# Relational graph convolution: loop edges taken from the nodes' own rows, the other edges closed up before the gather

## The chip, the cores and the metric

The kernel runs on one core of one Trainium2 chip. The metric is device time in microseconds (us), the median over runs. All engines of the core work side by side, each through its own instructions in order: TensorE (PE) multiplies matrices, VectorE (DVE) and ScalarE (ACT) work element by element, GpSimd (POOL) here only issues the gathers, and SyncE (SP) issues plain loads and stores.

## The reference, cut to what matters

A graph has 50000 nodes with 128 features each, and 850000 edges sorted by destination; 50000 of them are loops, one from each node to itself. Each edge has one of 16 types. Two layers of a relational graph convolution run one after the other, and the end is a residual and a layer norm:

```python
# one layer: h [50000, 128]; W[r] = sum over 8 bases of w_comp[r, b] * basis[b]
seg = dst * 16 + edge_type
agg = segment_sum(h[src], seg, 50000 * 16).reshape(50000, 16, 128)
msg = einsum('nri,rio->no', agg, W)
h = relu(msg + h @ loop_w + bias)
# after two layers
out = layernorm(x + h)
```

So the loop edges go through the typed matrices like all others, and besides them every node has the product with `loop_w`.

## The kernel before, in words

The edges are cut into tiles of 128 in the order of their destinations: 6641 tiles. Ten tiles (K) make a chunk, 665 chunks (C) per layer. The destinations of a tile lie within 12 nodes (WN), those of a chunk within 128.

A short set-up reads sources and destinations, 1024 tiles at a time (`looked_at`), transposes them on TensorE (L237) so that each edge of a tile has its own partition, and keeps them in SBUF for both layers: `src`, the row to gather, and `key`, the distance of an edge's destination from the first of its tile. It also works out where each chunk's nodes begin (`base_i`), how far the next chunk's are from them (`dist`), where each tile's 12 nodes lie in them (`slot`), and a flag `good` that says whether the edges fit this scheme. If they don't, `summed`, a general and slow path that neither version takes on these inputs, runs instead.

Then, for each layer and each chunk c:

- SP loads `hw`, the 128 rows of the chunk's own nodes (L430), in layer 2 also `xw` (L434).
- POOL gathers the source rows of ten tiles into `g`, one indirect DMA of 128 rows each (`gather`, L156). There are six buffers of ten tiles, so POOL runs up to six chunks ahead. Layer 1 gathers from x, layer 2 from H1, which layer 1 writes.
- Every fourth chunk, `weights` loads the edge types of 40 tiles (`rel`, L355), compares them with the type that each partition stands for (`is_rel`, DVE L364), and multiplies by the table of basis weights: `pm` (PE L367) then holds eight basis weights per edge.
- DVE makes `own`, one-hot over a tile's 12 nodes (L442), and `hot`, its product with `pm` (L449, 128x960).
- TensorE multiplies the gathered rows of each tile by `hot` (`pa`, L460, 128x96), ScalarE copies five tiles at a time to `aT` (L467).
- One chunk later (`finish`, called behind the first five tiles of the next chunk) `slots` sums eight products with the basis matrices (`ps`, L380; copied to SBUF as `slots`, L384), and `nodes_of` puts the 120 slots to their nodes with a one-hot matrix (`own` L390, `pn` L394), adds what the chunk before left for shared nodes (`shift` L397, `pn` L398, `kept` L400), transposes `hw` (`turned`, L163, copy `hT` L165), multiplies it by `loop_w` (`po`, L402), adds the bias (`s`, L404) and adds both (`pn`, L405).
- `ended` applies the relu and stores to H1 (L411, L412), or in layer 2 adds x, applies the norm (`normed`) and stores the output.

An f32 matmul appears in the profile as two instructions on TensorE. The framework sets the order of instructions on each engine when the program is built, and puts the semaphores; nothing is ordered by hand beyond the order of the calls and the numbers of buffers. SP carries loads and stores in one queue; the gathers have POOL's queue to themselves.

Of the kernel before, what the change touches and what calls it, by code (L numbers as in the profile page):

```python
# [31 lines left out]
U8 = mybir.dt.uint8  # L33
AF = mybir.ActivationFunctionType
# [5 lines left out]
P = 128  # L40
# [5 lines left out]
BATCH = 8  # L46
AT = 8
PER = 5
GATHERS = 6
# [9 lines left out]
def tile_rgcn_resnorm(  # L59
# [19 lines left out]
    n_tiles = -(-E // P)  # L79
    C = -(-n_tiles // K)  # L80
    assert D == P and N >= P and edges.shape[0] == 1 and AT * NR == P and PER * NB * WN <= BANK and AT * PER * NB <= BANK and K == 2 * PER and C >= 2 and E % ROW == 0
# [5 lines left out]
    H1 = dram.tile([N, D], F32, name="H1")  # L87

# [9 lines left out]
    fixed = ps_c.tile([P, 2, P], F32, name="fixed")  # L98
# [54 lines left out]
    ps_m = ctx.enter_context(tc.tile_pool(name="ps_m", bufs=2, space=PSUM))  # L153
# [20 lines left out]
    n_first = 0  # L174


    n_batches = -(-n_tiles // (P * BATCH))
    src = consts.tile([P, n_batches * P * BATCH], I32, name="src")
    key = consts.tile([P, n_batches * P * BATCH], F32, name="key")
# [3 lines left out]
    slot = consts.tile([P, C], F32, name="slot")  # L183
    good = consts.tile([1, 1], I32, name="good")
    with tc.tile_pool(name="meta1", bufs=1) as m1, tc.tile_pool(name="meta", bufs=2) as mp:
        ones = m1.tile([P, P], F32, name="ones")
        nc.vector.memset(ones, 1.0)

        def looked_at(i):

            raw = mp.tile([P, 2, BATCH, P], I32, name="raw")
            e0 = i * P * BATCH * P
            whole, part_of = divmod(min(E - e0, P * BATCH * P), BATCH * P)
            flat = raw.rearrange("p j b e -> p j (b e)")
            if whole < P:

                nc.vector.memset(flat[:, 0, :], 0)
                nc.vector.memset(flat[:, 1, :], N)
            for j in range(2):
                if whole:  # L200
                    nc.sync.dma_start(flat[:whole, j, :], column(j, e0, [[BATCH * P, whole], [1, BATCH * P]]))
                if part_of:
                    nc.sync.dma_start(
                        flat[whole : whole + 1, j, :part_of],
                        column(j, e0 + whole * BATCH * P, [[part_of, 1], [1, part_of]]),
                    )
            return raw

        raw = looked_at(0)

        first_i = m1.tile([K, C], I32, name="first_i")
        nc.vector.memset(first_i, N)
        with nc.allow_non_contiguous_dma(reason="one word in P"):
            nc.scalar.dma_start(first_i[:, : n_tiles // K], column(1, 0, [[P, K], [K * P, n_tiles // K], [1, 1]]))
            if n_tiles % K:
                nc.scalar.dma_start(  # L216
                    first_i[: n_tiles % K, C - 1 :],
                    column(1, (C - 1) * K * P, [[P, n_tiles % K], [1, 1], [1, 1]]),
                )
        picked = m1.tile([P, n_batches + 2], F32, name="picked")  # L220
        nc.vector.memset(picked, 0.0)
        for i in range(n_batches):
            if i:
                raw = looked_at(i)
            tb = mp.tile([P, BATCH], F32, name="tb")
            nc.vector.tensor_scalar(tb, raw[:, 1, :, 0], float(N - WN), None, op0=OP.min)
            rel0 = mp.tile([P, BATCH, P], F32, name="rel0")
            nc.vector.tensor_tensor(rel0, raw[:, 1], tb[:, :, None].to_broadcast([P, BATCH, P]), op=OP.subtract)
            srcf = mp.tile([P, BATCH, P], F32, name="srcf")
            nc.scalar.copy(srcf, raw[:, 0])  # L230
            t0 = i * P * BATCH
            for of, to in ((srcf, src), (rel0, key)):
                at = to[:, t0 : t0 + P * BATCH].rearrange("e (p b) -> e b p", b=BATCH)
                for b0 in range(0, BATCH, BANK // P):
                    tp = ps_a.tile([P, BANK], F32, name="pa")
                    for b in range(BANK // P):
                        nc.tensor.transpose(tp[:, b * P : (b + 1) * P], of[:, b0 + b, :], ident)  # L237
                    nc.scalar.copy(at[:, b0 : b0 + BANK // P, :], tp.rearrange("e (b p) -> e b p", p=P))
            while n_first < min(GATHERS, C - 1) and (n_first + 1) * K <= (i + 1) * P * BATCH:
                for k in range(K):  # L240
                    gather(rows[n_first][:, k, :], x, src[:, n_first * K + k : n_first * K + k + 1])
                n_first += 1
            own = mp.tile([P, BATCH, P], F32, name="own")
            nc.vector.tensor_scalar(own, rel0, 0.0, None, op0=OP.is_ge)
            nc.vector.scalar_tensor_tensor(
                own.rearrange("p b e -> p (b e)"),
                rel0.rearrange("p b e -> p (b e)"),
                float(WN),
                own.rearrange("p b e -> p (b e)"),
                op0=OP.is_lt,  # L250
                op1=OP.mult,
                accum_out=picked[:, i : i + 1],
            )
        tile_base = m1.tile([K, C], F32, name="tile_base")
        nc.vector.tensor_scalar(tile_base, first_i, float(N - WN), None, op0=OP.min)
        base1 = m1.tile([1, C], F32, name="base1")
        nc.vector.tensor_scalar(base1, tile_base[0:1], float(N - P), None, op0=OP.min)
        nc.vector.memset(base1[:, 0:1], 0.0)
        nc.vector.memset(base1[:, C - 1 :], float(N - P))
        nc.vector.tensor_copy(base_i, base1)  # L260

        spread = m1.tile([K, S], F32, name="spread")
        nc.gpsimd.iota(
            spread, pattern=[[1, S]], base=0, channel_multiplier=-WN, allow_small_or_imprecise_dtypes=True
        )
        ahead = m1.tile([K, S], F32, name="ahead")
        nc.vector.tensor_scalar(ahead, spread, 0.0, None, op0=OP.is_ge)
        nc.vector.scalar_tensor_tensor(spread, spread, float(WN), ahead, op0=OP.is_lt, op1=OP.mult)
        base = m1.tile([P, C], F32, name="base")
        within = m1.tile([P, 1], F32, name="within")  # L270
        po = ps_o.tile([P, D], F32, name="po")
        nc.tensor.matmul(po[:S, :1], spread, part[:K, :], start=True, stop=True)
        nc.vector.scalar_tensor_tensor(
            within[:S], po[:S, :1], float(-WN), part[:S], op0=OP.mult, op1=OP.add
# [58 lines left out]
    def chunked():  # L333
        with tc.tile_pool(name="hp", bufs=2) as hp, tc.tile_pool(
# [12 lines left out]
            def weights(c, n):  # L347
# [4 lines left out]
                if whole < AT:  # L352
                    nc.vector.memset(rel, NR)
# [270 lines left out]
    with tc.If(every > 0) as found:  # L624
        chunked()
# [41 lines left out]
```

## Time and profile before

| | us |
|---|---|
| median of 10 runs | 16696.05 (16694.3 to 16697.5) |
| profiled execution | 16664.61 |
| its span, first to last instruction | 16662.6 |
| POOL busy | 12559.0 |
| PE busy, weight loads | 13016.9, 11184.0 |
| DVE busy, ACT busy | 4001.6, 3111.7 |
| mean granted TensorE clock | 0.677 of full speed |

The busy time of an engine counts its instructions, and for the gathers POOL's own work only: the rows land later, under the DMA's name. A TensorE instruction's end is modelled, so its busy time is rough. The granted clock says how fast TensorE was let run. A group row of the profile gives the line, the engine, the operation, the tiles written and read, how often, busy us and mean ns; behind the second bar the idle time of the engine just before, and what ended it ("issue" if nothing that the profile shows). Times in a timeline are us from the start of the span. The DMA engines were busy for 20.6% with the gathers and 6.8% with SP's transfers.

### The profile page before, as it was taken

What the parts mean: (1) busy time and instruction counts of PE and PEld (TensorE: products, weight loads), DVE (VectorE), ACT (ScalarE), POOL (GpSimd) and SP (SyncE); (2) the same over time, 40 slices, a digit from 0 to 9 for tenths busy, and PEclk for the clock granted to TensorE, in tenths of its full rate; (3) what the DMA queues carried; (4) which work ended last, traced back from release to release, by engine and by line L of the source; (5) the groups of instructions that cost most, each with busy time, mean ns of one, the idle gap of its engine ahead of it and who ended that gap; (6) DMA issues with size and microseconds to landing.
All of it is one profiled execution on the core that took longest, in us unless ns stands there. A gap on an engine that the chain in (4) does not pass through costs nothing.

```text
span 16662.6 us, 191086 instructions
## 1 busy us (share of the span) xinstructions
PE 13016.9 (78%) x60630; PEld 11184.0 (67%) x60630; DVE 4001.6 (24%) x11719; ACT 3111.7 (19%) x8680; POOL 12559.0 (75%) x13290
## 2 busy tenths in 40 slices
PE   6777777777777777777777777778877787877788
PEld 5666666666666666666666666666666666666666
DVE  2222222222222222222222222222222222222222
ACT  2111111111111111111112122222222222222222
POOL 7777777777777777777777777777777777777777
PEclk7766666666666666666666666666666666666666
DMA  3222222222222222222222222222222222222222
GB/s 87 72 70 70 71 70 70 71 70 70 71 70 70 71 70 70 71 70 70 69 75 75 75 76 75 75 76 75 75 76 75 75 76 76 75 76 75 75 76 68
DMA packets 961778, 1218.82 MB, mean 73 GB/s; under 512 B 275684, under 2 KB 704100, under 8 KB 960768
## 3 DMA queue, kind: packets, MB, share of 16 engines
q0 software_dynamic: 425024, 871.30, 20.6%
q1 hardware_dynamic: 525876, 333.73, 6.8%
q8 instruction: 493, 8.08, 0.2%
q10 hardware_dynamic: 9868, 1.48, 0.1%
q14 instruction: 517, 4.24, 0.1%
HBM read 1118.27 MB, written 87.16 MB: 72 GB/s over the span
## 4 chain that ended last, share of the span: by engine, by line
DMA 50%; PE 30%; issue 15%; POOL 4%; POOLq 0%; ACT 0%; ACTq 0%; DVE 0%; SPq 0%
DMA g<-H,src 26%; DMA g<-in_x_dram,src 24%; PE pa L460 15%; PE ps L380 10%; POOL g L156 4%; PE pn L394 2%; PE pm L367 1%; PE pn L398 1%; PE po L402 1%; PE po L163 0%; POOLq L156 0%; ACTq L216 0%; DMA raw<-in_edges_dram 0%; ACT aT L467 0%; ACT o L330 0%
## 5 line engine op out<-in xcount | busy, mean ns | idle before, releaser
L460 PE MATMUL pa<-hot,g 128*128 128x96 f32 x26564 | 7569.7, 387 | 3586.0 <-DMA g<-in_x_dram,src 1834.4
L460 PEld LDWEIGHTS pa<-hot,g 128*128 128x128 f32 x26564 | 5705.4, 271 | 5378.5 <-DMA g<-H,src 2273.6
L156 POOL DMA_INDIRECT g<-in_x_dram,src x6641 | 6285.7, 946 | 2048.6 <-issue 951.4
L156 POOL DMA_INDIRECT g<-H,src x6641 | 6272.5, 945 | 2035.8 <-issue 801.6
L380 PE MATMUL ps<-basis,aT 128*120 128x128 f32 x21280 | 5524.1, 397 | 0.8 <-ACT aT L467 0.2
L380 PEld LDWEIGHTS ps<-basis,aT 128*120 128x120 f32 x21280 | 4602.9, 290 | 5.5 <-ACT aT L467 2.9
L467 ACT COPY aT<-pa 128x480 f32<-128x480 f32 x2658 | 1482.7, 558 | 8716.5 <-PE pa L460 8706.7
L390 DVE TENSOR_SCALAR own<-fixed,slot 120x128 f32<-120x128 f32 x1330 | 466.6, 351 | 10020.7 <-PE pn L394 10020.5
L449 DVE TENSOR_TENSOR hot<-pm,own 128x960 f32<-128x960 f32 x1330 | 1536.5, 1156 | 2025.3 <-PE pa L460 2002.6
L400 ACT COPY kept<-pn 128x128 f32<-128x128 f32 x1330 | 352.6, 265 | 2682.1 <-PE pn L398 2677.0
L402 PE MATMUL po<-loop,hT 128*128 128x128 f32 x2660 | 776.6, 386 | 3.7 <-ACT hT L165 2.4
L394 PE MATMUL pn<-slots,own 120*128 120x128 f32 x2660 | 702.6, 356 | 1.9 <-ACT slots L384 1.9
L398 PE MATMUL pn<-kept,shift 128*128 128x128 f32 x2656 | 653.0, 336 | 0.0
L367 PE MATMUL pm<-each,is_rel 128*128 128x64 f32 x3340 | 620.5, 310 | 3.4 <-DVE is_rel L364 3.4
L402 PEld LDWEIGHTS po<-loop,hT 128*128 128x128 f32 x2660 | 592.5, 275 | 25.5 <-ACT hT L165 23.9
L367 PEld LDWEIGHTS pm<-each,is_rel 128*128 128x128 f32 x3340 | 577.3, 238 | 3.6 <-issue 3.6
L394 PEld LDWEIGHTS pn<-slots,own 120*128 120x128 f32 x2660 | 555.0, 258 | 5.7 <-ACT slots L384 4.0
L398 PEld LDWEIGHTS pn<-kept,shift 128*128 128x128 f32 x2656 | 544.8, 254 | 0.2
L163 PE MATMUL po<-ident,hw 128*128 128x128 f32 x1330 | 470.2, 354 | 8.6 <-DMA hw<-H 4.4
L165 ACT COPY hT<-po 128x128 f32<-128x128 f32 x1330 | 353.7, 266 | 629.3 <-PE po L163 625.6
L397 DVE TENSOR_SCALAR shift<-fixed,dist 128x128 f32<-128x128 f32 x1328 | 459.4, 346 | 39.9
L404 DVE TENSOR_TENSOR s<-po,bias 128x128 f32<-128x128 f32 x1330 | 378.8, 285 | 288.7 <-PE po L402 276.3
(78 smaller groups left out, 3158.1 us busy)
## 6 DMA issues: line engine op xcount, KB each, us to landing
g<-in_x_dram,src POOLq DMA_INDIRECT x6641
g<-H,src POOLq DMA_INDIRECT x6641
rel<-in_edges_dram SPq DMA_DIRECT2D x332, 320.0 KB
hw<-in_x_dram SPq DMA_DIRECT2D x665, 64.0 KB
H<-h SPq DMA_DIRECT2D x665, 64.0 KB
hw<-H SPq DMA_DIRECT2D x665, 64.0 KB
xw<-in_x_dram SPq DMA_DIRECT2D x665, 64.0 KB
out_dram<-o SPq DMA_DIRECT2D x665, 64.0 KB
```

Of the source, the lines that this page charges most:

```text
L156: nc.gpsimd.indirect_dma_start(out=to, out_offset=None, in_=of, in_offset=bass.IndirectOffsetOnAxis(ap=idx, axis=0))
L163: nc.tensor.transpose(tp[:, :m], h, ident[:m, :m])
L367: nc.tensor.matmul(pm[:, :, j * NB : (j + 1) * NB], is_rel[:, j * P : (j + 1) * P], EACH[n], start=True, stop=True,)
L380: nc.tensor.matmul(ps[: k * WN], aT[:, b, : k * WN], BASIS[n][:, b, :], start=b == 0, stop=b == NB - 1)
L390: nc.vector.tensor_scalar(own[: k * WN], grid[: k * WN, :P], slot[: k * WN, c : c + 1], None, op0=OP.is_equal)
L394: nc.tensor.matmul(pn, own[: k * WN], st[: k * WN], start=True, stop=not c)
L397: nc.vector.tensor_scalar(shift, apart, dist[:, c - 1 : c], None, op0=OP.is_equal)
L398: nc.tensor.matmul(pn, shift, kept, start=False, stop=True)
L402: nc.tensor.matmul(po, turned(hw, P, sb), LOOP[n], start=True, stop=True)
L449: nc.vector.tensor_tensor(hot[:, :ks], pm[:, t0 : t0 + ks, :, None].to_broadcast([P, ks, NB, WN]), own[:, :ks, None, :].to_broadcast([P, k ...
L460: nc.tensor.matmul(pa[:, i * NB * WN : (i + 1) * NB * WN], g[:, k + i, :], hot[:, k + i].rearrange("e b w -> e (b w)"), start=True, stop=True,
L467: nc.scalar.copy(aT[:, :, k * WN : (k + m) * WN].rearrange("d b (i w) -> d i b w", w=WN), pa[:, : m * NB * WN].rearrange("d (i b w) -> d i ...
```

## The change

- The edges are cut into runs of 672 (RUN): 1265 of them. In each run, the loop edges are taken out and the others moved up to the front; of those there are at most 640, which make five tiles of 128 (HALF tiles, LIVE places). A chunk is two runs, as before ten tiles, and there are 633 chunks.
- The closing up (`closed_up`) is done by DVE on words that hold source, node and type of an edge: step b moves a word 2^b places if bit b of its distance, the number of loop edges ahead of it, is set. The test of the bit is a `tensor_scalar` from SBUF to PSUM, the move a masked copy within SBUF, 256 places at a time. `runs` does this for 128 runs and fills `src`, `key`, `slot`; the types go out to a small HBM tensor, REL, as bytes.
- `loops_of` does the opposite for the loop edges: it moves the type of each node's loop edge to the node's place, 128 chunks at a time, and writes it to LREL in HBM.
- Group 0 of both is done ahead. The other nine groups of runs and four of loops are generators: before each chunk of layer 1 one step of those under way is issued.
- `weights` loads REL and LREL instead of the edge types, makes one more small matmul into the same bank of PSUM, and returns `lw`, eight basis weights per node of the chunk for its loop edge.
- `loops` is new in every chunk: the transposed own rows times all eight basis matrices (two matmuls of 512 columns, `hb`), each times its basis weight per node (DVE, two products of 128x512), and the sum over the eight (DVE reduction, `ls`), which is added to `pn` ahead of `kept`.
- `ps_m` has one buffer instead of two, to make room for `ps_h`. `key` becomes bf16.
- The flag is now `bad` and is looked at behind both layers; `summed` would then write the output again.

```diff
-    n_tiles = -(-E // P)
-    C = -(-n_tiles // K)
+    R = -(-E // RUN)
+    C = -(-R // 2)
+    NG, NL = -(-R // P), -(-C // P)
...
-    ps_m = ctx.enter_context(tc.tile_pool(name="ps_m", bufs=2, space=PSUM))
+    ps_m = ctx.enter_context(tc.tile_pool(name="ps_m", bufs=1, space=PSUM))
+    ps_h = ctx.enter_context(tc.tile_pool(name="ps_h", bufs=1, space=PSUM))
...
+        first = pool.tile([1, C], I32, name="first")
+            nc.sync.dma_start(first, column(1, 0, [[1, 1], [2 * RUN, C], [1, 1]]))
...
+    def closed_up(word, low, last, bits, wanted=None):
+        for b in range(bits):
+            step = 1 << b
+            end = last - step
+            if wanted is not None:
+                end = min(end, wanted + (1 << bits) - (2 << b))
+            for a in range(0, end, 2 * P):
+                k = min(2 * P, end - a)
+                nc.vector.tensor_scalar(
+                    bit[:, :k], word[:, a + step : a + step + k], 1 << low + b, None, op0=OP.bitwise_and
+                )
+                nc.vector.copy_predicated(word[:, a : a + k], bit[:, :k], word[:, a + step : a + step + k])
+            yield
...
+    def runs(g, pool):
...
+        nc.scalar.copy(halves[:, :, 0], s_i)
+        nc.scalar.copy(quarters[:, :, 3], r_i)
+        loop = pool.tile([P, RUN], F32, name="loop_f")
+        nc.vector.tensor_tensor(loop, d_i[:, 1:], d_i[:, :RUN], op=OP.subtract)
+        nc.vector.scalar_tensor_tensor(quarters[:, :, 2], loop, 0.0, k_f, op0=OP.is_equal, op1=OP.mult)
...
+        yield from closed_up(word, 16, RUN, BITS)
...
+        put(srcf, src)
...
+        nc.vector.tensor_tensor(
+            keyf.rearrange("p (k e) -> p k e", e=P),
+            tiles,
+            begin[:, :, None].to_broadcast([P, HALF, P]),
+            op=OP.subtract,
+        )
+        nc.vector.scalar_tensor_tensor(keyf, place64, taken, keyf, op0=OP.subtract, op1=OP.max)
+        put(keyf, key)
+        rel8 = pool.tile([P, LIVE], U8, name="rel8")
+        nc.scalar.copy(rel8, quarters[:, :LIVE, 3])
+        nc.sync.dma_start(REL[r0 : r0 + P], rel8)
...
+    def loops_of(g, pool):
...
+        nc.vector.scalar_tensor_tensor(
+            away, d_i[:, :length], first, place, op0=OP.subtract, op1=OP.subtract
+        )
...
+        nc.vector.tensor_tensor(loop, d_i[:, 1:], d_i[:, :length], op=OP.subtract)
+        nc.vector.scalar_tensor_tensor(halves[:, :, 0], away, -1.0, loop, op0=OP.mult, op1=OP.mult)
+        yield from closed_up(word, 0, length, (length - 1).bit_length(), P)
...
+        nc.sync.dma_start(LREL[c0 : c0 + P], rel8)
...
     def weights(c, n):
-                rel = hp.tile([P, PER * P], I32, name="rel")
+                rel = hp.tile([P, LIVE], U8, name="rel")
...
+                is_l = hp.tile([Q * NR, P], F32, name="is_l")
+                nc.vector.tensor_scalar(is_l, lrel, its_rel[: Q * NR], None, op0=OP.is_equal)
...
+                nc.tensor.matmul(
+                    pm[:, AT * PER * NB :], is_l, EACH[n][: Q * NR, :Q, :], start=True, stop=True
+                )
+                lw = hp.tile([P, Q, NB], F32, name="lw")
+                nc.scalar.copy(lw, pm[:, AT * PER * NB :].rearrange("e (c b) -> e c b", b=NB))
...
+            def loops(c, hT, lw, n):
...
+                by = sb.tile([P, NB, D], F32, name="by", bufs=1)
+                few = BANK // D
+                for b in range(0, NB, few):
+                    hb = ps_h.tile([P, BANK], F32, name="hb")
+                    nc.tensor.matmul(
+                        hb, hT, BASIS[n][:, b : b + few, :].rearrange("p b d -> p (b d)"), start=True, stop=True
+                    )
+                    nc.vector.tensor_tensor(
+                        by[:, b : b + few, :],
+                        hb.rearrange("p (b d) -> p b d", d=D),
+                        lw[:, b : b + few, None].to_broadcast([P, few, D]),
+                        op=OP.mult,
+                    )
+                ls = sb.tile([P, D], F32, name="ls")
+                nc.vector.tensor_reduce(ls, by.rearrange("p b d -> p d b"), AX.X, OP.add)
+                return ls
...
+            def nodes_of(c, k, st, kept, hw, lw, n):
+                hT = turned(hw, P, sb)
+                ls = loops(c, hT, lw, n)
...
+                nc.vector.tensor_add(pn, pn, ls)
...
-                nc.tensor.matmul(po, turned(hw, P, sb), LOOP[n], start=True, stop=True)
+                nc.tensor.matmul(po, hT, LOOP[n], start=True, stop=True)
...
+            done(runs(0, pr))
+            done(rest_of_set_up)
...
                 for c in range(C):
+                    if n == 0:
+                        g, i = divmod(c, P // 2)
+                        if i == 4 and g + 1 < NG:
+                            some["runs"] = runs(g + 1, pr)
+                        if c == 0:
+                            done_loops = loops_of(0, pr)
+                        g, i = divmod(c, P)
+                        if i == P * 3 // 4 and g + 1 < NL:
+                            some["loops"] = loops_of(g + 1, pr)
+                        for of_kind in tuple(some):
+                            next(some[of_kind], None)
...
-    every = nc.values_load(good[0:1, 0:1], min_val=0, max_val=1)
-    with tc.If(every > 0) as found:
-        chunked()
-    with found.Else():
-        summed()
+    chunked()
+    wrong = nc.values_load(bad[0:1, 0:1], min_val=0, max_val=1)
+    with tc.If(wrong > 0):
+        summed()
```

## The prediction

> **What bounds the kernel now.** I first read the engine shares (part 1 of the page), then the group rows of the gather and of the two large matmul groups (part 5), then how the gathers follow one another in the timeline, and last the one stretch in which TensorE has a backlog. In a group row: busy us and mean ns of one, then the engine's idle time before it and what ended most of that.
>
> ```profile
> PE 13016.9 (78%) x60630; PEld 11184.0 (67%) x60630; DVE 4001.6 (24%) x11719; ACT 3111.7 (19%) x8680; POOL 12559.0 (75%) x13290
> ...
> L460 PE MATMUL pa<-hot,g 128*128 128x96 f32 x26564 | 7569.7, 387 | 3586.0 <-DMA g<-in_x_dram,src 1834.4
> ...
> L156 POOL DMA_INDIRECT g<-in_x_dram,src x6641 | 6285.7, 946 | 2048.6 <-issue 951.4
> L156 POOL DMA_INDIRECT g<-H,src x6641 | 6272.5, 945 | 2035.8 <-issue 801.6
> ```
>
> By shares TensorE looks like the bound: 78% against 75%. The group row speaks against it: TensorE sat idle for 3586 us ahead of the matmul `pa`, nearly all of it ended by the landing of gathered rows. The timeline of POOL, away from both ends, shows what sets the pace (start us, length us, then the idle time before the instruction in brackets):
>
> ```profile
> 5000.91 0.94 POOL L156 DMA_INDIRECT g<-in_x_dram,src  x1 [0.30 <-issue]
> 5002.16 0.94 POOL L156 DMA_INDIRECT g<-in_x_dram,src  x1 [0.30 <-issue]
> 5003.41 0.94 POOL L156 DMA_INDIRECT g<-in_x_dram,src  x1 [0.30 <-PE pa L460]
> 5004.66 0.94 POOL L156 DMA_INDIRECT g<-in_x_dram,src  x1 [0.30 <-PE pa L460]
> ```
>
> The gap is 0.30 us whatever releaser is named, so no engine is waited for: it belongs to the instruction, and POOL issues one gather per 1.25 us without rest. Its 75% is the whole of it. First and last gather of the layers start at 26.5 and 8334.8 us, and at 8347.8 and 16643.2 us, which gives 8308.3 / 6640 = 1.2513 us and 8295.4 / 6640 = 1.2493 us per gather. The span is 26.5 (before the first gather) + 8308.3 + 13.0 (between the layers; POOL waits for the last rows of H1) + 8295.4 + 19.4 (from the last gather's start to the end) = 16662.6 us. So a chunk of ten gathers has 12.5 us. What TensorE can do in them is seen where it has a backlog, after the set-up (columns: stretch, length, busy us of PE, PEld, DVE, ACT, POOL, then granted clock), and in two transposes, one per chunk, in that stretch:
>
> ```profile
> 80.00:110.00 30.00, 29.28 (x234) 28.81 (x234) 16.06 (x37) 9.92 (x28) 22.69 (x25) 0.89 0.41 105
> 110.00:150.00 40.00, 28.18 (x152) 25.29 (x150) 10.01 (x25) 7.17 (x21) 30.25 (x33) 0.76 0.28 73
> ```
>
> ```profile
> 93.24 0.27 PE L163 MATMUL po<-ident,hw 128*128 128x128 f32 x1
> 98.06 0.27 PE L163 MATMUL po<-ident,hw 128*128 128x128 f32 x1
> ```
>
> With work queued TensorE is granted 0.89 and needs 4.8 us for a chunk without `pm`, some 5.1 us with a quarter of the 1.25 us that its ten instructions took at 99.99 us. So TensorE has over 7 us a chunk to spare, and DVE (24% of 12.5 us is 3.0 us) over 9.
>
> **Part 1, the gathers.** 850000 edges are 1265 runs of 672, five gathers each: 6325 per layer for 6641. This part lies on the path that sets the end. Without the 7.6 us by which gathers of the set-up are longer than 0.94 us (summed from the timeline, 26 to 70 us), layer 1 has 1.2501 us per gather. New: 6324 x 1.2501 = 7905.6 us and 6324 x 1.2493 = 7900.6 us, for 8300.7 and 8295.4: a saving of 790 us. The waits ahead of a gather stay what they were (an earlier gather's landing, TensorE for the buffer six chunks back), with ScalarE's index copy added at two gathers of each group of 128 runs, and that copy is made some fifty chunks ahead.
>
> **Part 2, the loop edges, per chunk.** On TensorE two f32 matmuls of 512 columns (`hb`), two instructions each. No row of before has 512 columns. The nearest is `ps`, 128 columns, at full clock and at half:
>
> ```profile
> 8338.33 1.81 PEld L380 LDWEIGHTS ps<-basis,aT 128*120 128x120 f32 x16 [0.28 <-ACT aT L467]
> ...
> 16646.49 3.66 PE L380 MATMUL ps<-basis,aT 128*120 128x128 f32 x16
> ```
>
> That is 0.113 us each at full clock. If the weight load sets it, four more instructions cost 4 x 0.113 = 0.45 us; if the columns do, four times that, 1.8 us. I take 1.8, since a long stream of columns is what is added: 6.9 us a chunk at full clock, and even at the whole run's mean clock of 0.677, 10.2 us, below 12.5. In the built order the first `hb` stands three `pa` matmuls behind the transpose, which covers ScalarE's 0.27 us copy, and the second stands behind seven or so other matmuls, which covers DVE's product; once in four chunks the first cover is missing, for about 0.5 us. `pm` has one buffer for two: once in four chunks TensorE fills it only after the last `hot` that reads the old one, and `pa` then waits for `pm`, the copy `lw` and `hot`, some 3 us, or 0.8 per chunk. All of this is inside the 5 us left, and costs nothing as long as POOL's lead of six chunks stands; without that cover it would be about 0.9 us x 1266 = 1140 us.
>
> On DVE: two products of 512, from `hot` (960 elements, 1.156 us) 0.69 us each; the sum over the bases, 1024 elements, 1.22 us by the same slope; one addition, 0.30; `is_l` 0.1. With the 2.8 us of before 5.7 us in layer 1, and 6.8 with the norm of layer 2. Behind a DVE product that waits for `hb` stand `own` and `hot` of the next chunk, for which `pa` waits; they have over 5 us.
>
> DVE can touch the bound in another way: through the SBUF port it shares with POOL. The row first. In the set-up gathers grow, and some end 0.12 us after a DVE instruction does (41.29 after 41.17 here):
>
> ```profile
> 40.26 1.03 POOL L156 DMA_INDIRECT g<-in_x_dram,src  x1 [0.30 <-issue]
> ...
> 40.48 0.69 DVE L244 TENSOR_SCALAR own<-rel 128x1024 f32<-128x1024 f32 x1
> ```
>
> Over 26 to 70 us DVE ran about 23.6 us of instructions with all operands in SBUF, against the 7.6 us of growth: 0.32 us per us. Taken for the new sum over the bases, which has no PSUM operand, that is 1266 x 1.22 x 0.32 = 494 us lost. The Trainium skill, SBUF — State Buffer, section Who interferes with whom, says that a tensor_reduce on trn2 never contends, and that an instruction with at most one SBUF input outside the two-port modes doesn't: nothing lost. The rows lean to the page: in layer 2 `st` reads and writes SBUF in every chunk and the mean gather is 945 ns, not more than in layer 1. I take 0 and keep 494 for a rival. The two products read PSUM and one SBUF operand as `hot` does, which leaves gathers at 0.94 us.
>
> **Part 3, the closing up.** Ten groups of runs and five of loops, in layer 1 only, on DVE between chunks. Instructions with two SBUF inputs: eight of about 0.84 us (the 664-element row of the set-up) per group of runs and 4.9 us per group of loops: 67 + 25 = 92 us, at 0.32 some 30 us of gather growth. The masked copies, 10 x 18 + 5 x 52 = 440 of about 0.4 us, are 176 us; none is in the trace. Their mask lies in PSUM, so `hot` is nearest and I take 0; at 0.32 it would be 56. As load this adds at most 5 us to a chunk's 5.7 for some 25 chunks in 128, hidden in the 12.5. REL and LREL go to HBM and back, and `rel` falls from 320 KB to 80 KB; SP's queue does not bound, and POOL waits for none of its loads in layer 1.
>
> **Part 4, the ends.** Before the first gather DVE must now wait for the loads (about 8 us as before; the strided `first` perhaps 16), run 36 instructions of one group's closing (some 14 us) and about 7 us set among them; then ScalarE's copies and the transposes, 4 us. First gather at about 45 us (35 to 60) for 26.5. TensorE starts only when the first loop group is closed, some 75 instruction pairs later, at about 112 us; POOL's sixty-gather lead ends at about 45 + 75 + 8 = 128 us, so it is not stopped; 5 us for a miss, 25 at worst. Between layers 15 us for 13, and 22 for 19.4 at the end (the added sum and addition, and the check `bad` read at the end and not ahead).
>
> Sum: 45 + 7905.6 + 7900.6 + 30 + 5 + 15 + 22 = 15923 us of span. The profiled execution took 16664.6 us, 2.0 above its span, and the median of the runs is 31.4 above that; kept: **15957 us**, 4.4% less.
>
> **Rivals.** (a) *Every chunk's sum over the bases holds POOL's port*: 15957 + 494 = 16451 us, still faster. For it the set-up rows, against it `st` and the page. (b) *The closing up stops POOL*: DVE waits in order for loads of the next group, TensorE starves, and the sixty-gather lead is used up; nine groups at 20 us give 16137 us. Against it: 75 us of lead. (c) *TensorE becomes the bound*: if its clock stays at half while it starts and stops for `hT`, `hb` and `pm`, a chunk takes 2 x 6.9 = 13.8 us; 1266 x 13.8 + 119 (ends and set-up) + 33 = 17623 us. It decides from (16696 - 152) / 1266 = 13.07 us per chunk on. For it: the granted clock falls to 0.64 at the end, and 16 `ps` take 3.66 us there. Against it: 0.89 with a backlog, so a late TensorE gets faster. (d) *The fallback runs instead*: by the inputs each run has 35 to 44 loop edges (32 to 63 are allowed) and no tile spans over 12 nodes, so only an error would start it.
>
> **How the numbers follow.** Main case 0.80, (a) 0.07, (b) 0.05, (c) 0.07, (d) under 0.01. The main case's own range is 15895 (no growth of gathers, first gather at 35 us, no miss, shorter ends) to 16060 (56 us more growth, 15 more at the start, 20 at the miss, 10 at the ends). The range reaches over (b): 15890 to 16140; (a), (c) and a little of the main case stay outside, under 2 in 10. About 0.2% is what a measurement of this kernel tells from no change. Faster: 0.92; within 0.2%: 0.01; slower: 0.07.
>
> **What would show it.** Right: 12650 gathers with mean 945 to 952 ns and gaps of 0.30 us, 1.25 us from start to start in the middle of both layers; idle time ahead of `pa` still ended by gathered rows; TensorE busier at an equal or higher granted clock; DVE near half; the first gather near 45 us. Wrong: gaps before gathers beyond 0.30 us that end with `pa` (TensorE too late), gathers over 1 us throughout (the port), or a first gather far beyond 60 us.

## The result and the profile after

The changed kernel took 15950.92 us (median of 8 runs, 15947.64 to 15953.41) against 16695.69 us before (28 runs, 16690.61 to 16698.71): a ratio of 0.9554, 95% interval 0.9546 to 0.9562, so 4.5% faster. The forecast was 15957. On a second chip the changed kernel with one edit gives nearly the same ratio, 0.957 (e11). On three other chips, in e1 to e10, every kernel takes longer, and there the change made the kernel 2.2% slower (e10). Times are therefore compared only within one chip, and the sections below follow both findings.

The engine shares and the group rows of the changed kernel's page, in the columns described above:

```profile
PE 12362.2 (78%) x63470; PEld 9763.9 (61%) x63470; DVE 8213.1 (51%) x17689; ACT 2917.0 (18%) x8656; POOL 12008.8 (75%) x12661
...
L688 PE MATMUL pa<-hot,g 128*128 128x96 f32 x25300 | 5185.0, 321 | 3268.8 <-DMA g<-in_x_dram,src 1589.5
L173 POOL DMA_INDIRECT g<-in_x_dram,src x6325 | 6018.6, 952 | 1967.5 <-issue 1082.5
L173 POOL DMA_INDIRECT g<-H,src x6325 | 5987.3, 947 | 1947.9 <-issue 1084.1
...
L575 DVE TENSOR_TENSOR by<-hb,lw 128x512 f32<-128x512 f32 x2524 | 1740.8, 690 | 5115.9 <-PE hb L572 5099.4
L572 PE MATMUL hb<-basis,hT 128*128 128x512 f32 x5064 | 3231.8, 725 | 160.7 <-ACT hT L182 122.6
...
L582 DVE TENSOR_REDUCE ls<-by 128x128 f32<-128x1024 f32 x1266 | 2404.3, 1899 | 3.4
```

DVE's busy time doubled, TensorE got 5064 instructions of `hb` with 512 columns each, and still `pa` waits 3269 us, ended by gathered rows as before. POOL's share is again 75%, and its timeline is as even as it was, also from one layer to the next:

```profile
5001.74 0.95 POOL L173 DMA_INDIRECT g<-in_x_dram,src  x1 [0.30 <-PE pa L688]
5002.99 0.95 POOL L173 DMA_INDIRECT g<-in_x_dram,src  x1 [0.30 <-issue]
5004.24 0.94 POOL L173 DMA_INDIRECT g<-in_x_dram,src  x1 [0.30 <-DMA g<-in_x_dram,src]
...
7988.67 0.95 POOL L173 DMA_INDIRECT g<-in_x_dram,src  x1 [0.30 <-issue]
8009.16 0.95 POOL L173 DMA_INDIRECT g<-H,src  x1 [19.54 <-DMA H<-h]
```

The span of 15947.9 us is 42.7 (before the first gather) + 7946.0 (6324 x 1.2565) + 20.5 (between the layers) + 7914.7 (6324 x 1.2515) + 24.0 (end). So 632 gathers fewer at 1.25 us, 790 us, less what the ends and a slightly longer gather gave back. Counted over the whole trace, only two of the 12650 gathers have more than 0.33 us of idle time before them, the first of each layer; in the first profile of before it is also two, of 13282. Between the ends POOL is never held up in either kernel.

### The profile page after: what moved, and what is told of

The parts are those of the page before. It is cut to its first block, busy times and chain, and to the rows that moved or that the text cites. A ratio compares the mean times of both kernels' runs of the same rounds, so it can differ in the third digit from the quotient of the medians.

```text
span 15947.9 us, 201946 instructions
## 1 busy us (share of the span) xinstructions
PE 12362.2 (78%) x63470; PEld 9763.9 (61%) x63470; DVE 8213.1 (51%) x17689; ACT 2917.0 (18%) x8656; POOL 12008.8 (75%) x12661
## 4 chain that ended last, share of the span: by engine, by line
PE 46%; DMA 30%; issue 16%; POOL 4%; DVE 2%; ACT 1%; POOLq 0%; SPq 0%; ACTq 0%; DVEq 0%
DMA g<-in_x_dram,src 16%; PE ps L550 16%; DMA g<-H,src 14%; PE pa L688 12%; PE hb L572 11%; POOL g L173 4%; PE pm L532 2%; PE pn L594 2%; PE pn L598 2%; PE po L603 1%; PE po L180 1%; PE pm L539 1%; DVE ls L582 1%; DVE by L575 0%; ACT slots L554 0%
## 5 line engine op out<-in xcount | busy, mean ns | idle before, releaser
L688 PE MATMUL pa<-hot,g 128*128 128x96 f32 x25300 | 5185.0, 321 | 3268.8 <-DMA g<-in_x_dram,src 1589.5
L688 PEld LDWEIGHTS pa<-hot,g 128*128 128x128 f32 x25300 | 4144.3, 221 | 4543.4 <-DMA g<-in_x_dram,src 1992.5
L575 DVE TENSOR_TENSOR by<-hb,lw 128x512 f32<-128x512 f32 x2524 | 1740.8, 690 | 5115.9 <-PE hb L572 5099.4
L572 PE MATMUL hb<-basis,hT 128*128 128x512 f32 x5064 | 3231.8, 725 | 160.7 <-ACT hT L182 122.6
L550 PE MATMUL ps<-basis,aT 128*120 128x128 f32 x20256 | 3342.3, 334 | 11.4 <-ACT aT L695 11.0
L550 PEld LDWEIGHTS ps<-basis,aT 128*120 128x120 f32 x20256 | 3187.2, 241 | 49.8 <-ACT aT L695 25.1
L582 DVE TENSOR_REDUCE ls<-by 128x128 f32<-128x1024 f32 x1266 | 2404.3, 1899 | 3.4
L606 DVE TENSOR_TENSOR pn<-pn,s 128x128 f32<-128x128 f32 x1266 | 374.4, 296 | 1996.3 <-ACT kept L601 1988.6
L572 PEld LDWEIGHTS hb<-basis,hT 128*128 128x128 f32 x5064 | 917.4, 226 | 245.8 <-ACT hT L182 193.2
L554 ACT COPY slots<-ps 120x128 f32<-120x128 f32 x1266 | 338.2, 267 | 2301.0 <-PE ps L550 2294.0
```

The lines of the kernel that those rows point to most:

```text
L550: nc.tensor.matmul(ps[: k * WN], aT[:, b, : k * WN], BASIS[n][:, b, :], start=b == 0, stop=b == NB - 1)
L572: nc.tensor.matmul(hb, hT, BASIS[n][:, b : b + few, :].rearrange("p b d -> p (b d)"), start=True, stop=True)
L575: nc.vector.tensor_tensor(by[:, b : b + few, :], hb.rearrange("p (b d) -> p b d", d=D), lw[:, b : b + few, None].to_broadcast([P, few, D]) ...
L582: nc.vector.tensor_reduce(ls, by.rearrange("p b d -> p d b"), AX.X, OP.add)
L688: nc.tensor.matmul(pa[:, i * NB * WN : (i + 1) * NB * WN], g[:, k + i, :], hot[:, k + i].rearrange("e b w -> e (b w)"), start=True, stop=True,
```

## On a second chip, the work off the path moved (e11, e12)

These two bear on the main question: is POOL alone the bound? Both kernels have the same edit: what follows the slots is put off by one more chunk. In the changed kernel:

```diff
+                def begin(c, k, aT, hw, lw, n0, xw):
+                    return slots(c, k, aT, n), turned(hw, P, sb)
...
-                        if k == 0 and late is not None:
-                            kept = finish(kept, *late)
-                            late = None
+                        if k == 0:
+                            if begun is not None:
+                                kept = finish(kept, *begun)
+                                begun = None
+                            if late is not None:
+                                begun = begin(*late), *late
+                                late = None
```

> The changed kernel, with the second half of a chunk's work put off by one more chunk: the transposed own rows and the slots are made in the chunk behind (as now), but the products with them (hb, pn, po) only in the chunk after that. The work is the same. On the chips of the experiments TensorE stood 7582 us ahead of hb, mostly for the copy hT, which itself started late behind its product. If that round trip from TensorE to ScalarE and back is what the longer time there consists of (theory A), a chunk of distance takes it off: the wait ahead of hb falls below 2500 us, and the time from 19943 us to between 16000 us (12650 gathers at 1.25 us, and the ends) and 18500 us. If the signals are slow by their number (theory B), or TensorE's matmuls really take longer than the records say (theory C), the wait only moves to another line, and the time stays at 19700 to 20100 us.

> The kernel before, with the same putting off: slots and hT one chunk behind, pn and po two chunks behind. There the long wait on the chips of the experiments was pn for slots (4799 us). Theory A: it falls below 2000 us, and the time from about 19500 us to between 16700 us (13282 gathers at 1.25 us) and 18700 us; the changed kernel with the same edit is then the faster of the two by about as much as the gathers are fewer, 3 to 5%. Theories B and C: 19300 to 19700 us, and the changed kernel stays some 2% slower.

The chip that these two landed on is not one with the longer times, so the theories in the expectations, which concern those, stay untested by them. Measured: 15949.77 us for the changed kernel with the edit (ratio to the kernel before on this chip 0.957, 0.9554 to 0.9586), and 16664.44 us for the kernel before with it, against 16664.46 without (ratio 1.0, 0.999 to 1.0009). The edit moved TensorE's and ScalarE's waits about; in e11, for instance, the idle time ahead of `slots` and of `by` rose:

```profile
L575 DVE TENSOR_TENSOR by<-hb,lw 128x512 f32<-128x512 f32 x2524 | 1742.3, 690 | 6323.4 <-PE hb L572 6283.9
...
L554 ACT COPY slots<-ps 120x128 f32<-120x128 f32 x1266 | 335.2, 265 | 3130.6 <-PE ps L550 3129.7
```

The idle time was 5115.9 and 2301.0 us without the edit, and yet e12 and the kernel before agree to 0.1%, and e11 lies within 0.1% of what the changed kernel took on the other chip. So the waits that the edit moved are not on the path, and with POOL never held up the gain of 4.3 to 4.5% on these two chips is that of fewer gathers. The runs that leave gathers out (e2, e3, e9) all ran on the other three chips, so the price of a gather was not measured here by taking one away.

## The experiments on the three other chips

### The kernel before, gathers left out, the loop product left out (e1 to e4)

e1 is the kernel before, unchanged. Each of e1 to e8 is a single execution. The others in this section are the changed kernel with one edit each. e2 issues nine of each chunk's ten gathers and e3 five (the buffers are zeroed once, the rest of their rows are stale, all other work stays); e4 leaves out the product of the own rows with the eight bases, the loop edges' share.

```diff
+    for r in rows:
+        nc.vector.memset(r, 0.0)
...
-                    for k in range(ks):
+                    for k in range(min(ks, 9)):
```

```diff
-                ls = loops(c, hT, lw, n)
...
-                nc.vector.tensor_add(pn, pn, ls)
```

> The kernel before, unchanged, for a second profile of it. The prediction added 31.4 us between the profiled execution (16664.6 us) and the median of the runs (16696 us), and the changed kernel shows only 1.2 us there. If the first profile was a slightly quicker execution, this one has gathers of about 947 ns, as the changed kernel has in layer 2, and takes about 16695 us. If the 31 us belong to the kernel before, whatever its execution, its profile again shows gathers of 944 to 945 ns and about 16665 us.

> The changed kernel with nine of a chunk's ten gathers; the tenth tile's matmuls read old rows of the buffer (filled with zeros once), so part of the sums is wrong, and all other work stays. 632 gathers fewer per layer. Theory (POOL's issue of gathers sets the time): 1264 x 1.254 = 1585 us less, 14366 us. Rival (TensorE's chunk sets it): no change, 15950 us.

> The changed kernel with five of a chunk's ten gathers, the other tiles' matmuls on old rows. POOL would need 5 x 1.254 = 6.27 us a chunk. By the prediction TensorE needs 6.9 us a chunk when it has work queued, so it becomes the bound at about 1266 x 6.9 + 120 = 8860 us, with a granted clock of 0.95 or more. If DVE or the waits among the engines cost more than was estimated, the time is above 9000 us. If TensorE stayed at half clock while it starts and stops (the rival that ends slower), 13.8 us a chunk, 17600 us.

> The changed kernel without the per-chunk work for the loop edges: no products with the eight basis matrices, no weighting, no sum, no addition (the output lacks the loop edges' messages). Theory (that work is hidden behind the gathers): same time within 30 us, 15920 to 15955 us, and the same gather length in layer 2. Rival (the sum over the bases holds the port that POOL needs): gathers shorter and up to 494 us less.

On this chip the kernel before took 19357.7 us in e1 and 19354.5 beside it, 16% more than in the prediction's profile; e2 18458.35, e3 13779.45, e4 18603.21 us. The times expected were all for a pace of 1.25 us per gather, and all were missed, that of the unchanged kernel too. The group rows of e1 show that a single gather is as long as it was, but that POOL and ScalarE wait more, and that TensorE's `pa`, which waited 3586.0 us in the prediction's profile, hardly waits:

```profile
L156 POOL DMA_INDIRECT g<-H,src x6641 | 6287.7, 947 | 3387.5 <-issue 1327.0
L156 POOL DMA_INDIRECT g<-in_x_dram,src x6641 | 6298.0, 948 | 3333.7 <-issue 1311.7
L460 PE MATMUL pa<-hot,g 128*128 128x96 f32 x26564 | 5877.4, 335 | 64.9 <-issue 44.2
...
L467 ACT COPY aT<-pa 128x480 f32<-128x480 f32 x2658 | 1485.5, 559 | 10082.4 <-remote 6943.1
```

Per gather the two rows show 0.95 us of work and 0.51 us of idle time (3387.5 / 6641), where it was 0.31. So here TensorE has rows waiting for it, and not the other way round. A low clock is not the reason: the kernel before was granted 0.708 here against 0.677. "remote" stands where the profile found no maker for the signal that ended a wait. e2 and e3 then tell that on this chip the gathers are not simply the bound: per chunk (span / 1266) e2 took 14.58 us and e3 10.88 us, so four gathers are worth 3.70 us, 0.92 us each. With nine gathers POOL's own pace would need 9 x 1.25 = 11.3 us, with five 6.3; and e3 was granted a clock of 0.88, so it wasn't TensorE at half clock either. Gathers and the rest of the work largely add up here instead of running side by side. And e4 took 14.69 us per chunk against 14.55 in e1 (19355.6 / 1330): without the loop product the changed kernel is 3.9% faster than the kernel before here too; the chunks are 4.8% fewer (1266 / 1330).

### Both left out; the closing up, the test of the inputs, and the sum (e5 to e8)

e5 joins the edits of e3 (five gathers) and e4. e6 leaves the closing up out for all groups but the first (and fixes the flag `bad` at 0), so that sources, nodes and types of the later runs stay at their old places; e7 leaves out the part of `runs` that tests the inputs, for all groups but the first, with the same fixed flag; e8 lays the eight products out so that the sum reads neighbouring words.

```diff
-        yield from closed_up(word, 16, RUN, BITS)
+        if g == 0:
+            yield from closed_up(word, 16, RUN, BITS)
...
-        yield from closed_up(word, 0, length, (length - 1).bit_length(), P)
+        if g == 0:
+            yield from closed_up(word, 0, length, (length - 1).bit_length(), P)
```

```diff
+        if g:
+            return
```

```diff
-                by = sb.tile([P, NB, D], F32, name="by", bufs=1)
+                by = sb.tile([P, D, NB], F32, name="by", bufs=1)
...
-                        by[:, b : b + few, :],
+                        by[:, :, b : b + few].rearrange("p d b -> p b d"),
...
-                nc.vector.tensor_reduce(ls, by.rearrange("p b d -> p d b"), AX.X, OP.add)
+                nc.vector.tensor_reduce(ls, by, AX.X, OP.add)
```

> As the run with five gathers a chunk, and without the per-chunk work for the loop edges. TensorE then needs about 5.1 us a chunk and DVE about 3, POOL 6.27 us: by the theory POOL sets the time again, 2 x 3165 x 1.254 + 120 = 8060 us. The difference to the run with five gathers alone is what the loop edges' work would cost without its cover.

> The changed kernel in which only the first group is closed up: the bit tests and masked copies of the nine other groups of runs and four of loops are left out (other rows are gathered, as many as before; the flag is set to zero). The prediction put nothing for the masked copies: then the mean gather of layer 1 stays at 951 to 952 ns and the time within 10 us of the changed kernel's. If they held POOL as instructions with two SBUF inputs were reckoned to, 176 us x 0.32 = 56 us less, at most all of the growth that layer 1 shows over layer 2, about 30 us.

> The changed kernel without the four checking instructions of nine groups of runs (squares, equality, products; three of 672 elements and one of 640, all with two SBUF inputs; the flag is set to zero). If instructions with two SBUF inputs lengthen gathers by 0.32 us per us, 36 of about 0.84 us cost 10 us, and layer 1 has 10 us less of gather length. If such instructions do nothing, no difference.

> The changed kernel with the products stored feature by feature, the eight bases side by side, so that the sum over the bases reads neighbouring words instead of words 512 bytes apart. The sum took 1.90 us where 1.22 were estimated. If the stride is the cause, it falls to about 1.2 us, and the products, which now write with a stride, may get longer. The time stays the same within 10 us in any case, because DVE is hidden.

The kernel before took 19604.1 us on the chip of these four; e5 12042.89, e6 19874.46, e7 20036.56, e8 20056.68 us. As times, the last three are again far above the 15951 us of the prediction's chip. e7 and e8 differ by 0.1%, which tells nothing; e6 is 0.8 to 0.9% below both, and as a single execution tells little more. e5 takes 9.51 us per chunk. With e4 that is 1.04 us per gather and 4.3 us besides (the two chips are 1.3% apart); with the loop product, by e2 and e3, 0.92 us per gather and 6.3 us besides.

What can still be read is the length of single gathers, which is the same on these chips. Those of layer 1, where the closing up runs, and of layer 2 are in e6 (no closing up), e7 (no test) and e8 (both there):

```profile
L173 POOL DMA_INDIRECT g<-H,src x6325 | 5982.7, 946 | 3990.2 <-remote 1332.0
L173 POOL DMA_INDIRECT g<-in_x_dram,src x6325 | 6009.1, 950 | 3819.0 <-issue 1358.6
```

```profile
L173 POOL DMA_INDIRECT g<-in_x_dram,src x6325 | 6007.0, 950 | 3981.7 <-issue 1379.8
...
L173 POOL DMA_INDIRECT g<-H,src x6325 | 5982.8, 946 | 3990.6 <-remote 1336.3
```

```profile
L173 POOL DMA_INDIRECT g<-in_x_dram,src x6325 | 6008.7, 950 | 4046.3 <-PE pa L688 1362.3
L572 PE MATMUL hb<-basis,hT 128*128 128x512 f32 x5064 | 3918.1, 866 | 7716.2 <-ACT hT L182 7123.4
L173 POOL DMA_INDIRECT g<-H,src x6325 | 5982.5, 946 | 3944.8 <-remote 1330.2
...
L575 DVE TENSOR_TENSOR by<-hb,lw 128x512 f32<-128x512 f32 x2524 | 2745.0, 1088 | 4287.8 <-PE hb L572 2476.8
...
L582 DVE TENSOR_REDUCE ls<-by 128x128 f32<-128x1024 f32 x1266 | 1531.4, 1210 | 3.9
```

Layer 1 has 26.4, 24.2 and 26.2 us more gather time than layer 2. These differences alone decide little, since with all of the work in place e9 has 22.3 and e10 32.2 us. The traces tell more, gather by gather. In the changed kernel's first profile, layer 1 has 132 gathers over 10 ns longer than the median of 947, together 36.1 us. Sorted by what DVE did meanwhile: the 122 gathers during which one of the groups' long instructions with two SBUF inputs ran (0.8 to 1.7 us each, some 79 us in all) have 24.2 us of this; 286 others beside `is_rel` or `is_l` (L526, L528) 8.3 us; 606 others beside the bit tests or masked copies 3.4 us; the remaining 5311 have 0.2 us. In e6, without the closing up, the first of these shares is 23.6 us, in e8 20.9. So the masked copies cost gathers next to nothing, and the instructions with two SBUF inputs cost them about 0.31 us per us (24.2 / 79). e7 leaves out four of the eight such instructions of each later group of runs; its share is 18.9 us, at the low end of the 18.9 to 27.7 us of the runs that have them all, so it decides nothing.

e8 gives the price of the stride: the sum over neighbouring words takes 1210 ns, over words 512 bytes apart 1899; but then the products write with a stride and take 1088 ns for 690, and the three together need 3.39 us per chunk for 3.28.

### The change itself again, and runs of 674 (e9, e10)

e10 is the changed kernel, unchanged, timed against the kernel before on the third of these chips; e9 has runs of 674 edges, 6310 gathers per layer.

```diff
-RUN = 672
+RUN = 674
```

> The changed kernel with runs of 674 edges: 1262 runs, 6310 gathers per layer for 6325 (each run still has at most 640 edges that are no loops, and no tile spans more than 12 nodes). If POOL's issue sets the time, 30 gathers fewer are 30 x 1.254 = 38 us less than the changed kernel, 0.24%, about 15913 us. If the time is set by chunks (631 for 633), 4 x 12.5 = 50 us less at most.

> The changed kernel again, beside the one with runs of 674, for the difference between them: 15951 us.

The kernel before took 19519.13 us (9 runs), the changed one 19942.9 (5 runs, 19921.14 to 19969.81): ratio 1.0217, interval 1.0203 to 1.0231. e9 took 19892.71 us (19873.74 to 19912.14), ratio 1.019, interval 1.0177 to 1.0204. The 50 us between e9 and e10 are 0.25%; 30 gathers fewer at 1.25 us would be 37.5, and two chunks fewer in each layer at e10's 15.75 us (19941.0 / 1266) would be 63, so the run doesn't tell the two apart.

### Why the same kernels take longer there

POOL's stops make up the whole difference. In e10, 1527 gathers have more than 0.33 us of idle time before them, and beyond the usual 0.305 us all such time adds up to 4015 us, against 60 us in the changed kernel's first profile; the spans differ by 3993 us. And POOL stops because its buffers are full: when a gather of e10 starts, a median of 56 tiles are gathered and not yet multiplied, of the 60 that the six buffers hold; in the first profile it is 2. So TensorE's side is late, and the question is why. Three timelines of e10 over one stretch in which a chunk is held up, of POOL, of TensorE and of ScalarE:

```profile
6014.10 0.94 POOL L173 DMA_INDIRECT g<-in_x_dram,src  x1 [0.30 <-issue]
6015.35 0.94 POOL L173 DMA_INDIRECT g<-in_x_dram,src  x1 [0.30 <-issue]
6018.68 0.94 POOL L173 DMA_INDIRECT g<-in_x_dram,src  x1 [2.39 <-remote]
```

```profile
6011.91 0.27 PE L180 MATMUL po<-ident,hw 128*128 128x128 f32 x1
6012.02 0.81 PE L688 MATMUL pa<-hot,g 128*128 128x96 f32 x6
6018.86 2.08 PE L572 MATMUL hb<-basis,hT 128*128 128x512 f32 x2 [6.03 <-ACT hT L182]
```

```profile
6018.37 0.27 ACT L554 COPY slots<-ps 120x128 f32<-120x128 f32 x1 [7.30 <-remote]
6018.53 0.27 ACT L182 COPY hT<-po 128x128 f32<-128x128 f32 x1
```

TensorE ended the transpose `po` at 6012.18 us. ScalarE, free, began the copies of `ps` and `po` only at 6018.37, and TensorE waited for them. POOL meanwhile issued gathers up to 6015.35, then stopped for a buffer that TensorE had to give back; the rows of the last one landed by 6017.6. And only then, at 6018.35 to 6018.51 us, the trace has five signals of TensorE's (updates of the semaphore by which it tells the others that an instruction is done) within 0.16 us. This is frequent in e10: 660 times three or more of its signals come within 0.12 us behind a gap of over 3 us, in nine of ten cases 2.7 to 3.9 us after the last gather began, and POOL's next gather begins 0.34 us behind them (median). e1 has 171 such cases; the changed kernel's first profile and the first of before have none; the nearest two signals of TensorE's are 109 ns apart there (one matmul), while in e10 23% and in e1 31% come less than 60 ns after the one before. Matmuls that begin 109 ns apart or more should not end so, which speaks against a slower TensorE as the cause and for signals that exist and are held back; since the ends of matmuls are modelled, this is argued and not shown.

Only TensorE's signals are seen to arrive late. Where ScalarE was free when the last `ps` ended, it began `slots` over 1 us later in 40% of 499 cases in e10, and in none of 1240 in the first profile. From the end of `hT` on ScalarE to a waiting `hb`, in contrast, it took a median of 52 ns in e10 and 51 ns in the first profile, and from `kept` to DVE's addition 33 ns in both.

They aren't held back by slower transfers either: the rows of a gather end 2.21 us (median) after it begins, in e10 as in the first profile. What else differs is that the traces of these chips hold fewer updates of semaphores. One of the gathers' shows 26532 in the first profile of before (16 for each of its 1661 gathers) and 5083 in e1, some three each; TensorE's shows 26078 and 21803, DVE's 11669 and 5353. Whether several updates are told as one there, or records are missing, the traces don't say.

So the picture that fits the runs is this: on those three chips many of TensorE's signals don't get through while gathers follow one another, and do when POOL stops. Of the recorded ones, 38% in e10 and 27% in e1 come when the last gather began over 2 us ago, which holds for 15% and 7% of the time; the rest come while gathers are issued. POOL's buffers stay nearly full, it stops for the next one to be given back, the held signals arrive, TensorE's chain moves on by a chunk, and POOL gets ten more gathers: in e10 the stops of over 1 us lie 5, 10 or 15 gathers apart in nearly nine of ten cases. So gathers and chain largely add up, which is what e2, e3, e4 and e5 measured. Why these chips do it, and those of e11 and of the first profiles do not, no run shows. A distance of one more chunk (e11, e12) was meant to test the remedy and landed on a chip of the other group; whether it helps stays open.

The price of the change there can be split up by per-chunk times, scaled to e1's chip (x 19354.5 / 19519.1): 64 chunks fewer x 14.55 us = 931 us gained; other work in a chunk, e4 less e1, 1266 x 0.14 = 177 us lost; the loop product, 15.75 x 0.992 - 14.69 = 0.93 us, x 1266 = 1177 us lost. The sum is 423 us slower, 2.2%; it has to agree with e10, which is one of its terms, so it shows the shares and proves nothing more, and e4 ran on another chip than e10. Hidden behind POOL the loop product cost nothing; where it isn't hidden, it costs more than all that the fewer chunks bring. The waits of e10 show where:

```profile
PEld hb L572 <- ACT hT L182: 7164.0, 1053, 15.7
PE hb L572 <- ACT hT L182: 6945.2, 1052, 15.5
ACT slots L554 <- remote: 5274.5, 897, 18.2
```

(The line that waits and for what, then total us, how often, the longest.) With no chunk's distance between `hT` and `hb`, TensorE waits for a round trip through ScalarE, 1052 times in 1266 chunks; in the first profile the same wait was 122.6 us.

## Why the prediction was right, point by point

- *POOL's issue is the bound.* Right for the chip predicted on: 0.30 us before all gathers but two, whoever is named, and e11 and e12 unchanged to 0.1% with the waits of the other engines moved. It was argued from one chip's profile, though, and on three other chips it doesn't hold.
- *Part 1, the gathers.* The pace was given as 1.2501 and 1.2493 us, plus 30 us of growth in layer 1; measured 1.2565 and 1.2515. Growth apart, both are some 2 ns up. The profiled execution of before that the pace was taken from was a quicker one: its median gather is 944 ns, where the changed kernel has 947 in its first profile, in e10 and in e11, and the kernel before has 947 in e1. On e11's chip twelve of thirteen runs of before lie at 16662 to 16670 us, and one at 16697; so before runs at one of two levels, 32 us, or 2.4 ns per gather, apart. The 31.4 us that were carried over from the profile to the median are the same size; that they are this level of the gathers is argued, since no profile of before at the higher level on those chips is there. In the changed kernel's profiled execution it is inside the gathers (15949.72 us, median 15950.92). The span was 25 us short and the carried offset 30 too much: most likely one quantity, put in the wrong place. That the total is only 6 us off is in part luck.
- *The port and the sum over the bases.* The sum took 1899 ns and not 1.22 us, since it reads with a stride (1210 ns without, e8). At 0.32 us per us the rival would now say 769 us lost. Layer 2 has a sum in each chunk, and its mean gather is 947 ns, with only 37 gathers over 975 ns, together 4.9 us above the median. Nothing is lost, as the Trainium skill's page SBUF — State Buffer, section Who interferes with whom, has it, and the set-up's 0.32 doesn't carry over to this instruction.
- *Part 3, the closing up.* The growth of 30 us in layer 1 came out as 31 (951.6 less 946.6 ns, x 6325), and mostly for the reason given. In the trace the instructions with two SBUF inputs carry 24.2 of the 36.1 us by which its long gathers exceed the median, at 0.31 us per us (0.32 taken), and their time was 79 us where 92 were reckoned. The masked copies (460, 401 to 404 ns each, as estimated) cost the gathers next to nothing, as taken. What the sum put at nothing is `is_rel` and `is_l`, 8.3 us; before has it too, where long gathers beside `is_rel` make up 7.8 us of layer 1.
- *TensorE and DVE have room.* DVE came to 51%, 6.5 us of a chunk (5.7 and 6.8 predicted for the two layers). The granted clock rose from 0.677 to 0.823. At full clock one `hb` begins 0.43 us after the other (591 ns is the length of one, and the next begins before its end), so four take 1.7 us a chunk, where 1.8 was taken: the columns set it, not the weight load. All was under POOL's 12.5 us.
- *The ends.* First gather at 42.7 us (45), between layers 20.5 (15), end 24.0 (22). The errors nearly cancel: with the 5 us for a miss the ends were put at 87 us and took 87.2. POOL wasn't stopped by the late start of TensorE, whose first `pa` began at 114.8 us.
- *The rivals.* (a) and (b) did not occur. (c), that TensorE's side becomes the bound and the change then loses, did, but on other chips and by another mechanism: not through a low clock (0.754 in e10, against 0.71 for before on the same chip), but, as argued above, through signals that arrive late. What the prediction gave as the price without cover, 0.9 us a chunk, was summed from `pm` and the copy `hT`; e4 and e10 give 0.93 us for the loop product, which is another quantity, so that the two agree is chance.

## What to carry to other kernels

Where one engine issues at a fixed gap whoever is named as releaser, count its instructions: fewer of them is the gain, and all else is free as long as its lead stands. But ask what each added piece of hidden work costs if the cover is gone: a zero that rests on cover was a zero on two chips here and 0.93 us a chunk by e4 and e10 on others. A chunk's distance between a product, its copy and the next product cost nothing where it ran (e11, e12); whether it helps on the other chips is untested. And before an offset between one profiled execution and the median is carried over, take a second profile and look for the instruction whose median length differs.

## What was not expected of the hardware

- The same program took 16664 or 16696 us on two chips and 19354, 19604 and 19519 us on three others, with gathers of the same length (944 to 947 ns median) and the same time to landing; on those, many of TensorE's signals came in bunches when the gathers paused.
- The change's sign depends on it: a ratio of 0.9554 on the first chip, 1.0217 on the one of e10.
- A reduction over words 512 bytes apart took 1899 ns for 1024 elements per partition, over neighbouring ones 1210; a product that writes with a stride of 32 bytes 1088 ns for 690.
- The median length of a gather of 128 rows was 944 ns in some executions and 947 in others, on chips of both groups.
- Gathers grew by about 0.31 us per us of DVE instructions with two SBUF inputs that ran beside them, and next to nothing beside masked copies whose mask lies in PSUM (3.4 us over 606 gathers).
